# Attention over a graph: degree rows moved into the middle places, checks, roundings and loads of strips at fixed steps of the last place

## The chip, the cores and the metric

The kernel runs on one core of one Trainium2 chip. The metric is the device time of one execution in microseconds (us). The engines of a core are PE (TensorE: matmuls and transposes; PEld is its weight load), DVE (VectorE), ACT (ScalarE), POOL (GpSimd) and SP (SyncE, which here issues DMAs). Each engine works through its own queue in a fixed order, and an instruction that waits holds up those behind it on the same engine.

## The reference

Two layers on a graph of 2708 nodes with 128 features. `adj` is a 0/1 matrix of 2708 x 2708. Shortened:

```python
# layer 0
deg = clip(adj.sum(axis=1), 1.0);  dis = deg ** -0.5
diffusion = (dis[:, None] * adj * dis[None, :]) @ x - x
sim  = x @ x.T / (norms[:, None] * norms[None, :])
attn = softmax(beta * sim * adj, axis=1)
x = layernorm(x + diffusion + sigmoid(alpha) * (attn @ x - x))
# layer 1
XW = x @ W;  s_col = XW @ a[0, :128];  s_row = XW @ a[0, 128:]
den = exp(leaky_relu(s_row[:, None] + s_col[None, :], 0.01))
num = adj @ den
att = where(num != 0, den / num, 0)
x = layernorm(x + adj @ (att @ XW))
```

## The kernel before

The kernel has a version for adjacencies that a low precision holds exactly, `grouped` (which is what runs here), and a general one behind a condition. Whether the condition holds is found out on the way: ACT sums the absolute values of the low 16 bits of the adjacency's numbers (`low_bits_of`, `check_part`). These are the "checks".

Rows are handled in 22 blocks of 128, columns in strips of 512 (`SW`), six of them with the last one short (148, `SHORT`; strip number `NS - 1` = 5, the "side" strip). Row blocks lie in groups of four; group 5 has only two blocks.

**The attention part** (to about 219 us) walks five places, `for n, s in enumerate(order)` at L579 with `order = (2, 3, 4, 1, 0)`: place 0 works on strip 2, place 3 on strip 1 together with the side strip (it is the wide one), and place 4, the last, on strip 0. In each place there are 22 steps `k`, over row blocks in the order `taken`: blocks 8 to 21, then 4 to 7, then 0 to 3. So groups 2, 3, 4, 5, 1, 0 have their steps one after another. One step is:

- PE: `sim`, a matmul of 128 x 512 (or four transposes, where an earlier place has kept the turned block),
- DVE (L212 in the profile, a helper's line): `p_t = sim * gentle * pieces`, where `pieces` are blocks of the strip of the adjacency,
- ACT (L217): `p_t = exp(p_t + shift)`,
- POOL (L222): `total += p_t`, the softmax's denominators,
- PE (L207): `att_acc += x_sb^T p_t`, started one or more steps later. `p_t` has six buffers.

Beside the steps other work is laid into the loop:

- `degree(ib, h)`: half a block row of the adjacency is loaded by a DMA on SP into one of three rooms (`row0`, `row1`, and a part of `x1`), and ACT sums it by a copy with an accumulator (L198, `row<-row` or `x<-x`, 128 x 1354). There are 44 of these "degree rows"; `rows_at` says at which steps of which place they are asked for. `roots(b0, b1)` makes `dis` from them (DVE and POOL).
- `round_part(g)` at `rounded_at[g]` of the last place: DVE copies group g of strip 0 into the format fp32r for the diffusion.
- `check_part(g)` at `checked_at[g]` of the last place: the check of group g's numbers on ACT; its output, which nobody reads, goes into `row0` or `row1`, the same rooms that degree rows land in. Groups 1 and 0 are not in that table; they are checked later, in the diffusion's first pass, into a room of their own (`low_junk`).
- `load_part(1, g)`: POOL's queue asks for group g of strip 1 as fp32r, for the diffusion. It lands in the tile that held strip 0's group, so it stands behind what reads that one. At k = 17 and 20 of the last place groups 2 and 3 are asked for, the others in the diffusion's first pass.
- After steps 11, 15, 19 and 21 of the last place `x_sb` is scaled by `dis` on DVE (L742), for those blocks whose `att_acc` matmul lies behind. Then `halves` (L795) splits it into `x_hi` and `x_lo` (DVE, L212).

`pinned` chains instructions of one engine: each is put behind the last pinned one. `in_order(f)` sets the chain's end to the latest step's instruction (`behind`) and pins everything that `f` issues. What is not pinned is placed by a scheduler at compile time, by its own estimates of durations. Either way each engine's queue is fixed when the kernel is built, and rests on dependences through the rooms as well.

**The diffusion part** (to about 330 us) runs over strips, `for s in (NS - 1, 0, 1, 2)` at L1014 and then strips 3 and 4. `diffuse(s, acc)` is 22 x 2 matmuls on PE (`dif_acc<-strip,x_hi` and `dif_acc<-strip,x_lo`, L207; for the side strip `dif_acc<-side,x_sb`). `attended(s, acc, total)` closes a strip's attention: eight small matmuls make row sums of `total` (`sums`, L528), `att_acc` is copied to SBUF by ACT (`to_sbuf`) and turned on PE (`tr_ps`), and DVE divides and adds into `att`. For strip 0 this stands in the first pass, s = 5, that is between the side strip's diffusion and strip 0's. Afterwards each strip is normalized and layer 1's scores are made. Jobs of the next stage (`fill`) with their own loads (`nat`, issued by SP at L829) are laid in between from about 283 us. Layer 1 itself runs from about 345 us to the end.

Of the kernel before, what the change touches and what calls it, by code (L numbers as in the profile page):

```python
# [12 lines left out]
I16 = mybir.dt.int16  # L13
# [5 lines left out]
P = 128  # L19
N = 2708  # L20
D = 128
NB = (N + P - 1) // P
NP = NB * P
LAST = N - (NB - 1) * P
SW = 512
# [22 lines left out]
def grouped(  # L48
# [15 lines left out]
    nc = tc.nc  # L64
# [10 lines left out]
    def width(s):  # L75
        return min(SW, N - s * SW)

    def blocks(s):
        return min(SW // P, NB - s * (SW // P))
# [114 lines left out]
    def pinned(engine, op, *args, **kwargs):  # L194
        with ExitStack() as e:
            if engine in latest:
                e.enter_context(tc.issue_after(latest[engine].ins))
            latest[engine] = op(*args, **kwargs)  # L198
            return latest[engine]
# [14 lines left out]
    def act(op, *args, **kwargs):  # L214
        if strict:
            return pinned("ACT", getattr(nc.scalar, op), *args, **kwargs)
        return getattr(nc.scalar, op)(*args, **kwargs)  # L217

    def gps(op, *args, **kwargs):
        if strict:  # L220
            return pinned("POOL", getattr(nc.gpsimd, op), *args, **kwargs)
        return getattr(nc.gpsimd, op)(*args, **kwargs)  # L222
# [12 lines left out]
    def to_sbuf(acc, v, nb):  # L235

        t = lp.tile([P, SW], F32, tag="to_rows", name="tr_sb", bufs=2)
        if v < nb * P:
            nc.gpsimd.memset(t[:, v : nb * P], 0.0)
        act("copy", t[:, :v], acc[:, :v])  # L240
        return t
# [8 lines left out]
    def turned(t, nb):  # L250

        rows = tp_bank("tr_ps")
        for b in range(nb):
            mm(nc.tensor.transpose, rows[:, b, :], t[:, ts(b, P)], ident)
        return rows
# [38 lines left out]
    groups = list(dict.fromkeys(b // 4 for b in taken))  # L294
# [39 lines left out]
    with ExitStack() as es:  # L334
        pz = pool("pz", EARLY + 3, side="right", stack=es)
        pa = pool("pa", side="right", stack=es)
        row_rooms = [pa.tile([P, N // 2], F32, name=f"row{k}") for k in range(2)]
# [158 lines left out]
        def in_order(f):  # L496

            latest.update(behind)
            strict.append("some")
            f()  # L500
            strict.pop()
# [13 lines left out]
        def roots(b0, b1):  # L515

            t = deg[:, b0:b1]
            dve("tensor_tensor", t, deg2[:, b0:b1, 0], deg2[:, b0:b1, 1], ALU.add)
            dve("tensor_scalar", live[:, b0:b1], t, 0.0, None, ALU.is_gt)
            dve("tensor_scalar", t, t, 1.0, None, ALU.max)  # L520
            gps("tensor_tensor", dis[:, b0:b1], t, minus_half[:, b0:b1], ALU.pow)

        def attended(s, acc, total):

            v, nb = width(s), blocks(s)
            sums = tp_bank("sums")
            for b in range(nb):
                nc.tensor.matmul(  # L528
                    sums[:, b, 0:1], total[:, ts(b, P)], ones[:, 0:1], start=True, stop=True
                )  # L530
            rsum = small.tile([P, SW // P], F32, tag="rsum", name="rsum")
            nc.vector.reciprocal(rsum[:, :nb], sums[:, :nb, 0])
            nc.vector.tensor_scalar(rsum[:, :nb], rsum[:, :nb], sig, None, ALU.mult)
            rows = turned(to_sbuf(acc, v, nb), nb)
            for b in range(nb):
                ib = s * 4 + b
                r = att[:, ib, :]
                nc.vector.scalar_tensor_tensor(
                    r, rows[:, b, :], rsum[:, b : b + 1], r, ALU.mult, ALU.add
                )  # L540


        room_of = {2: "room5", 3: "room1", 4: "room3", 1: "room0", 0: "room4", 5: "room2"}
        rounded_at = {2: 5, 3: 8, 4: 12, 1: 15, 0: 18, 5: 19}
        checked_at = {2: 13, 3: 18, 4: 21, 5: 21}
        strips = {0: {}, NS - 1: kept_c}

        def part_of(s, g):
# [7 lines left out]
        def round_part(g):  # L556
            dve("tensor_copy", part_of(0, g), kept_a[g])

        def check_part(g, room=None):
            low_bits_of(  # L560
                kept_a[g].rearrange("p b i -> p (b i)"),
                room or row_rooms[g % 2].bitcast(I16),
            )

        def load_part(s, g):
            src = adj_t[4 * g * P : min(4 * g + 4, NB) * P, ts(s, SW)]
            pinned(
                "strips", gps, "dma_start", part_of(s, g),
                src.rearrange("(b p) i -> p b i", p=P),
            )  # L570
# [6 lines left out]
        ended = []  # L577
        scaled = set()
        for n, s in enumerate(order):  # L579
            wide = n == side_n  # L580
            w_all = SW + SHORT if wide else SW
            acc = ps_acc.tile([P, SW], F32, tag="acc", name="att_acc")
            if wide:
                total = x1[:, :6, :].rearrange("p b i -> p (b i)")
                nc.gpsimd.memset(total[:, w_all:], 1.0)
                tp_tags.remove("tp2")
                acc_side = ps_tp.tile([P, SW], F32, tag="tp2", name="att_acc_side")
            else:
                total = lp.tile([P, SW], F32, tag="total", name="total", bufs=2)
            gps("memset", total[:, :w_all], 0.0)  # L590

            prep = {
                (0, 1): lambda: normalize(12, 16),
# [6 lines left out]
                (1, 17): lambda: constants(2),  # L600
                (2, 11): lambda: roots(0, 8),
                (3, 20): lambda: roots(8, 18),
                (4, 12): lambda: roots(18, NB),
            }

            rows_at = {
                0: (18, 20), 1: range(0, NB, 2), 2: range(0, NB, 2),
                3: [k for k in range(21) if k % 3 < 2], 4: range(0, 12, 2),
            }
            turns = {  # L610
                3: lambda: turn_rows(12, 16, by_dve),
# [20 lines left out]
            for k, jb in enumerate(taken):  # L632
# [91 lines left out]
                if n == len(order) - 1:  # L724
                    for g in [g for g, at in rounded_at.items() if at == k]:
                        in_order(lambda: round_part(g))
                    if k in (17, 20):
                        in_order(lambda: load_part(1, groups[k > 17]))
                    for g in [g for g, at in checked_at.items() if at == k]:
                        in_order(lambda: check_part(g))  # L730
                    if k in (11, 15, 19, 21):

                        done = sorted(taken[: k + 1 if k == NB - 1 else k - 1])
                        done = [b for b in done if b not in scaled]
                        scaled.update(done)
                        while done:
                            b0 = b1 = done[0]
                            while b1 in done:
                                done.remove(b1)
                                b1 += 1  # L740
                            xs = x_sb[:, b0:b1, :]
                            nc.vector.tensor_tensor(  # L742
                                xs, xs,
                                dis[:, b0:b1].unsqueeze(2).to_broadcast([P, b1 - b0, D]),
                                ALU.mult,
                            )
# [8 lines left out]
    work2 = pool("work2", 2, stack=es)  # L755
# [6 lines left out]
    low = late.tile([P, NB], F32, name="low")  # L762
# [72 lines left out]
    for q in range(4):  # L835
        i, end = KEPT * SW + q * quarters[1], KEPT * SW + (q + 1) * quarters[1]
        c = 0
        while i < end:
            s = min(i // SW, NS - 1)
# [174 lines left out]
    for s in (NS - 1, 0, 1, 2):  # L1014
        acc = ps_acc.tile([P, SW], F32, tag="acc", name="dif_acc")
        diffuse(s, acc)
        if s < 3:
            load_strip(s + 2)
        if s == NS - 1:
            attended(*ended.pop())  # L1020
            for g in (1, 0):
                check_part(
                    g, work2.tile([P, 2048], I16, tag="low", name="low_junk", bufs=1)
                )
            for g in groups[2:]:
                load_part(1, g)
        if s == 1:
            flat = kept_c.rearrange("p b i -> p (b i)")
            v = SHORT
            for b0, b1 in ((0, NB // 2), (NB // 2, NB)):  # L1030
                low_bits_of(
                    flat[:, b0 * v : b1 * v],
                    work2.tile([P, 2048], I16, tag="low", name="low_junk", bufs=1),
                )
        normed(s, summed_up(s, acc))
        x1_t = x1_in_sbuf(s, x1_turned(s))
        pbs = []
        for k in (1, 0):
            pb = scores(s, x1_t, k, score_bank())
            tally(s, pb, k)  # L1040
            pbs.append(pb)
        shared_row(s, pbs[0])
        picked(s, pbs[0], sr_p)
        picked(s, pbs[1], sc_p)
        limited(s * 4, s * 4 + blocks(s))
        e2(s * 4, s * 4 + blocks(s))
        if s == 1:
            fill("e")

    r, s = NS - 3, NS - 2  # L1050
# [4 lines left out]
    acc = ps_acc.tile([P, SW], F32, tag="acc", name="dif_acc")  # L1055
# [70 lines left out]
    for name in "kj":  # L1126
        t = tmp.tile([P, 2, NB, 32], F32, tag=name + "_ons", name=name + "_ons")
# [402 lines left out]
    for step in range(NG + LAG):  # L1530
        g, before, first = step, step - 1, step - LAG
# [94 lines left out]
    k = 0  # L1626
# [568 lines left out]
```

## Time and profile before

| | us |
|---|---|
| median of 3 runs (lowest, highest) | 651.85 (651.62, 652.48) |
| the profiled execution: its own time | 652.04 |
| the profiled execution: span in the profile | 649.3 |

| engine | busy us | share of the span | instructions |
|---|---|---|---|
| PE | 608.8 | 94% | 2859 |
| DVE | 491.4 | 76% | 978 |
| ACT | 471.3 | 73% | 649 |
| POOL | 289.2 | 45% | 270 |

Times inside the profile are microseconds from the start of the span; a row of the timeline begins with the start and the duration. A duration in a row holds some pipelining, so that the distance between two starts is often a little shorter than the duration; such a distance is called a pitch here. "x10" at the end of a row is a number of instructions put together in one row; brackets tell how long the engine was idle before and who ended it. A name such as `row<-row` is the output tile and the input tiles. The mean granted clock of PE over the whole span was 0.984 of full speed. The places of the attention begin at about 10, 48, 92, 130 and 174 us.

### The profile page before, as it was taken

To read this page: it belongs to the slowest core of one execution; us is meant where nothing else is said; L and a number is where in the kernel's file an instruction comes from. 1 tells how busy PE (TensorE), PEld (TensorE's weight loads), DVE (VectorE), ACT (ScalarE), POOL (GpSimd) and SP (SyncE) were. 2 spreads that over 40 slices of the span, in tenths; PEclk is the share of its full clock that TensorE was granted. 3 is DMA by queue.
4 is the path that set the end of the run, shared out by engine and by line. 5 is a ranking of instruction groups with operands and counts; after the bars stand their busy time and mean duration, and the time that the engine had idled before them with its cause. 6 is when DMAs were issued, how large, how long until landed. Compare 5 with 4: busy or idle time off the path is not lost.

```text
span 649.3 us, 8555 instructions
## 1 busy us (share of the span) xinstructions
PE 608.8 (94%) x2859; PEld 351.9 (54%) x2859; DVE 491.4 (76%) x978; ACT 471.3 (73%) x649; POOL 289.2 (45%) x270
## 2 busy tenths in 40 slices
PE   7999999999999899998878899999999999989993
PEld 4445345465655676765664344444444444658872
DVE  5765865764699756756885999899999999599575
ACT  4767786767889521410585999999999999778652
POOL 6967778777798742000123322333232230021573
PEclk9999999999999899999988999999999999999997
DMA  8968989988971999989956999756689453259981
GB/s 270 392 221 330 317 301 363 360 329 310 335 262 70 276 390 389 387 267 375 394 205 185 238 223 246 214 168 175 193 217 267 170 170 129 87 202 383 390 320 53
DMA packets 66407, 171.64 MB, mean 264 GB/s; under 512 B 10059, under 2 KB 19285, under 8 KB 63333
## 3 DMA queue, kind: packets, MB, share of 16 engines
q1 hardware_dynamic: 42500, 107.01, 46.4%
q0 software_dynamic: 22464, 62.25, 34.5%
q10 hardware_dynamic: 1392, 1.77, 0.8%
q8 instruction: 24, 0.39, 0.2%
q14 instruction: 27, 0.21, 0.1%
HBM read 171.89 MB, written 5.72 MB: 274 GB/s over the span
## 4 chain that ended last, share of the span: by engine, by line
PE 65%; ACT 13%; DVE 10%; POOL 6%; issue 4%; DMA 1%; another core or an unknown queue 0%; DVEq 0%; POOLq 0%; ACTq 0%
PE num L198 11%; PE m_acc L198 11%; PE att_acc L207 9%; PE h_acc L1690 7%; PE sim L207 7%; PE dif_acc L207 6%; ACT q L198 5%; POOL total L222 4%; ACT L198 2%; DVE q L198 2%; PE tot L198 2%; PE dif_acc L198 1%; PE sim L198 1%; POOL ss L198 1%; ACT xn L198 1%
## 5 line engine op out<-in xcount | busy, mean ns | idle before, releaser
L198 PE MATMUL m_acc<-q,xws 128*128 128x512 f32 x240 | 121.6, 592 | 0.0
L198 PE MATMUL num<-ring,wt 128*128 128x512 f32 x216 | 98.2, 546 | 3.6 <-DVE q L198 2.2
L222 POOL TENSOR_TENSOR total<-total,p_t 128x512 f32<-128x512 f32 (+1 forms) x67 | 91.8, 1370 | 21.0 <-ACT p_t L217 18.4
L207 PE MATMUL att_acc<-p_t,x_sb 128*128 128x512 f32 x184 | 91.1, 602 | 1.1 <-ACT p_t L217 1.1
L212 DVE SCALAR_TENSOR_TENSOR p_t<-sim,gentle,pieces 128x512 f32<-128x512 f32 x89 | 65.0, 746 | 34.8 <-PE sim L207 25.7
L198 DVE SCALAR_TENSOR_TENSOR q<-sr_b,nc_s,q 128x1536 f32<-128x1536 f32 (+1 forms) x48 | 77.8, 1623 | 17.3 <-ACT q L198 17.3
L217 ACT ACTIVATE p_t<-p_t,shift 128x512 f32<-128x512 f32 (+1 forms) x89 | 64.7, 745 | 33.8 <-DVE p_t L212 31.5
L198 DVE COPY q<-num 128x512 f32<-128x512 f32 (+1 forms) x142 | 83.5, 611 | 4.5 <-PE num L198 4.5
L198 PEld LDWEIGHTS m_acc<-q,xws 128*128 128x128 f32 x240 | 45.3, 190 | 55.0 <-issue 54.8
L198 ACT ACTIVATE q<-q,head,rest 128x1536 f32<-128x1536 f32 (+1 forms) x48 | 70.2, 1508 | 1.6 <-DVE ring L198 1.3
L198 ACT ACT_TABLE_LOAD x52 | 66.7, 1283 | 3.9 <-issue 3.1
L198 PEld LDWEIGHTS num<-ring,wt 128*128 128x128 f32 x216 | 39.0, 190 | 49.1 <-issue 34.2
L198 ACT ACTIVATE q<-q,c_s 128x1536 f32<-128x1536 f32 (+1 forms) x48 | 62.9, 1355 | 0.3
L198 POOL DMA_INDIRECT ring<-in_adj_t,k_no x18 | 20.8, 1154 | 89.1 <-PE num L198 85.6
L207 PEld LDWEIGHTS att_acc<-p_t,x_sb 128*128 128x128 f32 x184 | 31.7, 189 | 35.3 <-ACT p_t L217 18.8
L207 PE MATMUL sim<-xn_t 128*128 128x512 f32 x98 | 47.6, 592 | 0.0
L222 POOL TENSOR_TENSOR x<-x,p_t 128x660 f32<-128x660 f32 (+1 forms) x22 | 35.1, 1596 | 11.3 <-ACT p_t L217 10.6
L198 ACT ACTIVATE row<-row 128x1354 f32<-128x1354 f32 x30 | 39.5, 1318 | 0.3 <-DMA row<-in_adj 0.3
L207 PE MATMUL dif_acc<-strip,x_hi 128*128 128x512 f32 x88 | 37.8, 429 | 0.0
L207 PE MATMUL dif_acc<-strip,x_lo 128*128 128x512 f32 x88 | 36.2, 411 | 0.0
L1690 PE MATMUL h_acc<-rounded,m_hi 128*128 128x512 f32 x88 | 32.4, 407 | 3.7 <-DVE rounded L212 3.7
L198 PE MATMUL num<-x_sb,wt 128*128 128x512 f32 (+1 forms) x72 | 34.4, 570 | 0.7 <-ACT gb L198 0.7
(362 smaller groups left out, 1170.6 us busy)
## 6 DMA issues: line engine op xcount, KB each, us to landing
pieces<-in_adj_t SPq DMA_DIRECT2D x24, 1024.0 KB, 6.8
strip<-in_adj_t POOLq DMA_DIRECT2D x20, 1024.0 KB, 18.3
row<-in_adj SPq DMA_DIRECT2D x30, 677.0 KB, 5.5
nat<-in_adj_t SPq DMA_DIRECT2D x19, 768.0 KB, 7.7
x<-in_adj SPq DMA_DIRECT2D x14, 677.0 KB, 6.2
ring<-in_adj_t SPq DMA_DIRECT2D x9, 1024.0 KB, 5.1
pieces<-in_adj_t SPq DMA_DIRECT2D x7, 512.0 KB, 6.4
x_sb<-in_adj_t SPq DMA_DIRECT2D x4, 768.0 KB, 6.2
```

The lines of the kernel that those rows point to most:

```text
L198: latest[engine] = op(*args, **kwargs)
L207: op(*args, **kwargs)
L212: return getattr(nc.vector, op)(*args, **kwargs)
L217: return getattr(nc.scalar, op)(*args, **kwargs)
L222: return getattr(nc.gpsimd, op)(*args, **kwargs)
L1690: nc.tensor.matmul(acc[:, : rows.shape[-1]], m[:, kb, :], rows, start=(kb, part) == (0, 0), stop=(kb, part) == (NB - 1, 1),)
```

## The change

- `rows_at`: place 1 asks for one more degree row (at k = 21), place 2 for two more (at k = 5 and 13), the last place for three instead of six (k = 0, 2, 4). `roots(18, NB)` goes from k = 12 to k = 7 of the last place.
- `rounded_at` is earlier by one step (group 5) to four steps (groups 4, 1 and 0).
- `checked_at` names all six groups, each at the step behind its rounding; the two checks with `low_junk` in the diffusion are gone, and `check_part` writes to `row0` or `row1` always.
- `asked_at` is new: all six groups of strip 1 are asked for at steps of the last place, each behind the group's check, in place of two there and four in the diffusion.
- The two `memset`s of the wide place's `total` are pinned.
- `attended` for strip 0 is called behind `diffuse(0)` instead of ahead of it; the copy of `att_acc` to SBUF stays ahead of it.

```diff
-        def attended(s, acc, total):
+        def attended(s, acc, total, t=None):
...
-            rows = turned(to_sbuf(acc, v, nb), nb)
+            rows = turned(t or to_sbuf(acc, v, nb), nb)
...
-        rounded_at = {2: 5, 3: 8, 4: 12, 1: 15, 0: 18, 5: 19}
-        checked_at = {2: 13, 3: 18, 4: 21, 5: 21}
+        rounded_at = {2: 3, 3: 5, 4: 8, 1: 11, 0: 14, 5: 18}
+        checked_at = {2: 4, 3: 6, 4: 9, 1: 12, 0: 15, 5: 19}
+        asked_at = {2: 9, 3: 10, 4: 13, 1: 16, 0: 19, 5: 21}
...
-        def check_part(g, room=None):
+        def check_part(g):
             low_bits_of(
                 kept_a[g].rearrange("p b i -> p (b i)"),
-                room or row_rooms[g % 2].bitcast(I16),
+                row_rooms[g % 2].bitcast(I16),
             )
...
-                nc.gpsimd.memset(total[:, w_all:], 1.0)
+                in_order(lambda: gps("memset", total[:, w_all:], 1.0))
...
-            gps("memset", total[:, :w_all], 0.0)
+            if wide:
+                in_order(lambda: gps("memset", total[:, :w_all], 0.0))
+            else:
+                gps("memset", total[:, :w_all], 0.0)
...
-                (4, 12): lambda: roots(18, NB),
+                (4, 7): lambda: roots(18, NB),
...
-                0: (18, 20), 1: range(0, NB, 2), 2: range(0, NB, 2),
-                3: [k for k in range(21) if k % 3 < 2], 4: range(0, 12, 2),
+                0: (18, 20), 1: (*range(0, NB, 2), 21), 2: (*range(0, NB, 2), 5, 13),
+                3: [k for k in range(21) if k % 3 < 2], 4: (0, 2, 4),
...
-                    if k in (17, 20):
-                        in_order(lambda: load_part(1, groups[k > 17]))
                     for g in [g for g, at in checked_at.items() if at == k]:
                         in_order(lambda: check_part(g))
+                    for g in [g for g, at in asked_at.items() if at == k]:
+                        in_order(lambda: load_part(1, g))
...
         if s == NS - 1:
-            attended(*ended.pop())
-            for g in (1, 0):
-                check_part(
-                    g, work2.tile([P, 2048], I16, tag="low", name="low_junk", bufs=1)
-                )
-            for g in groups[2:]:
-                load_part(1, g)
+            in_sbuf = to_sbuf(ended[0][1], SW, SW // P)
+        if s == 0:
+            attended(*ended.pop(), in_sbuf)
```

The compiled queues of the two kernels differ in this way around the last place. ACT: before, degree rows stand among steps 1 to 15, the check of group 2 ahead of step 16's exponential, that of group 3 behind step 18's, those of groups 4 and 5 behind step 21's. After, one row stands ahead of step 0, seven among steps 3 to 15; behind step 16's exponential stand the check of group 2, the last degree row, and the checks of groups 4, 3, 0 and 1; then the exponentials of steps 17 to 19, the check of group 5, and those of steps 20 and 21. DVE: behind step 21's product stand the scaling of blocks 18 to 21, that of blocks 4 to 7, seven of the splits, and the scaling of blocks 0 to 3. POOL: the asks for groups 2, 3, 4 and 1 stand between the additions of steps 16 and 17, that of group 0 behind step 19's, that of group 5 at the end. PE: strip 0's `att_acc` matmuls of steps 17 to 21 stand behind most of the side strip's diffusion; then the last side matmuls, strip 0's 44, and only then `sums`.

## The prediction

> **What bounds the kernel now.** I read the page's busy tenths first (PE, TensorE, near nine nearly everywhere, with a dent a third of the way in), then the busy time of each engine by windows. Columns: window, length, busy time and instructions of PE, its weight loads, DVE (VectorE), ACT (ScalarE) and POOL (GpSimd), granted clock, DMA share, GB/s.
>
> ```profile
> 48.00:92.00 44.00, 43.99 (x130) 20.44 (x129) 31.75 (x63) 32.83 (x51) 32.13 (x27) 1.00 0.87 310
> 92.00:130.00 38.00, 37.69 (x126) 19.16 (x125) 24.84 (x44) 27.73 (x43) 30.43 (x25) 1.00 0.99 359
> 186.00:200.00 14.00, 13.86 (x55) 7.52 (x55) 13.82 (x20) 13.39 (x21) 12.59 (x7) 1.00 0.71 237
> 200.00:210.00 10.00, 8.69 (x33) 4.82 (x31) 8.87 (x12) 10.00 (x13) 8.12 (x7) 1.00 0.00 0
> 210.00:218.60 8.60, 6.06 (x32) 4.39 (x32) 6.84 (x5) 4.74 (x9) 8.38 (x8) 1.00 0.52 132
> 231.00:270.00 39.00, 39.00 (x180) 28.09 (x179) 27.53 (x146) 11.45 (x18) 9.61 (x13) 1.00 1.37 388
> ```
>
> In the middle places PE is full and ACT has a quarter of its time free; in the second half of the last place ACT is full (10.00 of 10.00); from 219 on PE is full again. So work put into the middle is covered, and ACT work put into the last place is paid. Next, the chain of waits around the last place's end, then PE's own timeline there:
>
> ```profile
> 212.02 1.27 POOL total L222
> 217.28 1.29 POOL total L222
> 218.62 1.08 PE sums L528 x8
> 219.70 0.53 PE tr_ps L207 x2
> 220.23 4.28 PE dif_acc L207 x13
> ```
> ```profile
> 213.17 2.68 PE L207 MATMUL dif_acc<-side,x_sb 128*128 128x148 f32 x20
> 218.62 1.08 PE L528 MATMUL sums<-ones,total 128*128 128x1 f32 x8 [2.55 <-POOL total L222]
> 219.88 0.78 PE L207 MATMUL dif_acc<-strip,x_hi 128*128 128x512 f32 x1
> ```
>
> POOL's last addition lets `sums` go, and strip 0's diffusion starts at 219.88. From there to 272 the waits show PE waiting once, 0.7 us; the strip loads wait for PE (`POOL strip <- PE dif_acc`, 14.8 us in 10 waits). The loads after it are tied to PE as well (the queue at L829 waits 33.4 us for PE). I therefore carry a shift of 219.88 in full to the end.
>
> **The change part by part.** The diff alone would say "checks spread over the place". What decides is ACT's compiled queue, which is a fixed order. A check writes the room that degree rows land in, so it must stand behind every row ordered before it, and the queue still has nine of the 44 rows in the last place, the final one behind step 16. In the changed queue one row stands ahead of step 0, seven among steps 0 to 16, and no check; then stand, without an exponential between them: check of group 2, the last row, checks of groups 4, 3, 0, 1; then p17, p18, p19, the check of group 5, p20, p21 (p17 is step 17's exponential). Before, one check stood ahead of p16, one ahead of p19, two behind p21, and the two of groups 1 and 0 in the diffusion at 216.06 and 218.10. ACT's rows of before:
>
> ```profile
> 199.66 1.32 ACT L198 ACTIVATE row<-row 128x1354 f32<-128x1354 f32 x1
> 200.97 1.90 ACT L198 ACTIVATE row<-pieces 128x2048 int16<-128x2048 int16 x1
> 202.86 1.94 ACT L217 ACTIVATE p_t<-p_t,shift 128x512 f32<-128x512 f32 x3
> 204.70 1.90 ACT L198 ACTIVATE row<-pieces 128x2048 int16<-128x2048 int16 x1
> 206.60 1.93 ACT L217 ACTIVATE p_t<-p_t,shift 128x512 f32<-128x512 f32 x3
> 210.32 1.05 ACT L198 ACTIVATE row<-pieces 128x1024 int16<-128x1024 int16 x1
> ```
>
> Starts give the pitches: row 1.31, check 1.89, three exponentials 1.84 to 1.94, so 0.61 each; p17 started at about 203.5.
>
> *When p16 is ready.* Its product on DVE stood at 199.75 before. DVE now has one more rounding cast ahead (1.2) and spends 0.7 of idle time on it: about 200.3. ACT: p15 from 199.6, a row 1.32, p16 0.61, so free at 202.1. *The clump:* 1.89 + 1.32 + 4 x 1.89 = 10.77 us. p17 starts at 212.9, 9.4 later than before.
>
> *Behind p17.* Exponential and matmul 0.72 + 0.86, with 0.1 of hand-over; then DVE, whose next operation is the scaling of blocks 4 to 7 and which waits for that matmul, with the splitting into x_hi and x_lo queued behind it, though most blocks were long scaled. By before's rows:
>
> ```profile
> 213.37 0.69 DVE L742 TENSOR_TENSOR x_sb<-x_sb,dis 128x512 f32<-128x512 f32 x1 [1.76 <-PE att_acc L207]
> 213.97 2.90 DVE L212 CAST x_hi<-x_sb 128x384 fp32r<-128x384 f32 x2
> 216.80 2.92 DVE L212 TENSOR_TENSOR x_lo<-x_sb,x_hi 128x384 fp32r<-128x384 f32 x2
> 219.65 0.92 DVE L212 CAST x_hi<-x_sb 128x768 fp32r<-128x768 f32 x2
> 220.48 1.54 DVE L212 TENSOR_TENSOR x_lo<-x_sb,x_hi 128x768 fp32r<-128x768 f32 x2
> ```
>
> Scaling 0.69; the first four splits 5.7 (2.90 + 2.92 less overlap, beside POOL's additions, as they will again be); the next casts and a difference, which the queue puts ahead of the last scaling, 1.8 (the rows at 219.65 and 220.48, nothing beside them) to 3.6 (beside POOL, double); I take 2.4, nearer the first, since POOL is nearly through. Last scaling 0.69, the last four side matmuls 1.0 at 0.25. Sum 12.1: strip 0 starts at 225.0.
>
> *Moved work.* The row sums and two transposes (218.62 to 219.88, 1.26 us) now stand behind strip 0: still PE work, no gain. Strip 0's matmuls start 5.1 later, and what follows 5.1 + 1.26 = 6.4 later. Sums of totals cost no wait there: they are ready by about 222, and wanted after strip 0's 10 us; if not, 0 to 2.
>
> *The clock.* Before, PE idled 2.55 us, and strip 0's first matmuls ran at half clock:
>
> ```profile
> 220.00:221.00 1.00, 1.00 (x5) 0.81 (x4) 1.00 (x3) 0.97 (x3) 1.00 (x2) 0.50 1.27 420
> ```
>
> Seven matmuls at a pitch of 0.43 instead of 0.23 lost 1.4 us. Now there are two idle stretches, about 4 us ahead of p17's matmul and 4 to 5 us ahead of strip 0. The first falls where PE waits for others anyway; the second replaces the one of before. I add 0.4 for slower side matmuls and transposes between; bounds 0 and 1.4. [...]
>
> *At nothing.* Three rows more in middle places: 3 x 1.32 = 4.0 us of ACT under full PE (ACT 32.83 of 44 and 27.73 of 38). Their DMAs stand ahead of pieces on SP, where place two's share is 0.99; two rows are 1.39 MB, at 359 GB/s 3.9 us if that cover is gone, bounded at 0 and 3.9; I take 0, as pieces are asked for a place ahead, over 30 us. Memsets moved on POOL: under 1 us. Strip-1 asks: the four behind the clump wait for checks on POOL and delay additions; POOL issues each in 0.8 to 1.0, some 3.3 us, covered by strip 0, since nothing but the sums waits for totals. Earlier strips bring nothing while PE is the bound.
>
> Total: 6.4 + 0.4 = 6.8. The profiled execution has a span of 649.3 and took 652.04, 2.74 around it; 649.3 + 6.8 + 2.74 = 658.8, and the median lies 0.19 under that run: **658.6**.
>
> **The rivals.**
> **A, faster: ACT is quick enough.** ACT's work from p0 up to p17 is 17 x 0.61 + 8 x 1.31 + 5 x 1.89 = 30.3. Were p0 to start at 174.8 as before and nothing to wait, p17 would start at 205.1, strip 0 at 217.2, and with 1.26 moved behind it the end would come 1.4 earlier: 650.4; with p17 at 203.5, as before, 648.8. It decides when p17 starts ahead of 206.5 (206.5 + 12.1 + 1.26 = 219.9). Against: DVE was busy 13.82 of 14.00 us ahead of step 16, so p16 can't come 7 us earlier. 0.08.
> **B, no change: the checks run at their steps** (the rooms free sooner, or ACT idles less than I read): with the row now ahead of p0 and some idle time p0 starts at 176.6, p17 at 207.0, +0.5, 652.4. Against: the queue is fixed. 0.04.
> **C, strip 1's earlier loads repay it:** asks at about 204 to 213 instead of 211 to 222; if diffusion were fed by DMA (388 GB/s), up to 6 come back: 653 to 655. Against: PE full, 39.00 of 39.00. I give it 0.06 of the forecast's chance, at its lower end.
> [...] 0.12.
>
> **How the numbers follow.** Forecast 0.76, around 658.6. Its ends: with the splits unhindered (2.1 instead of 5.7), -3.6; with p17 1.2 earlier, another -1.2, so 653.8; I go to 653.5. Above: the slow differences +1.2, clock +1.0, part of the places' 3.9: 662.5. About 1 in 10 lies out on each side. This kernel's measurement can tell 0.2%, 1.3 us, from no change: faster 0.08 (A), same 0.04 (B), slower 0.88 (forecast and D).
>
> **What would show it.** Right: in ACT's timeline five checks and one row back to back from about 202 to 213, and p17 at 213; two idle stretches of PE, ahead of `att_acc` and ahead of the first `dif_acc<-strip` near 225; clock near 0.5 behind the second; `sums` behind strip 0. Wrong: p17 ahead of 206.5, exponentials between the checks, idle PE in places one and two, or PE waiting less in 225 to 330 than before.

## The result, and the profile after

| | before | after |
|---|---|---|
| median, us (lowest, highest; 6 runs each) | 651.74 (649.58, 652.93) | 658.81 (656.99, 663.03) |
| the profiled execution: its own time | 652.04 | 659.52 |
| the profiled execution: span | 649.3 | 657.8 |

The ratio of the times is 1.0124, 95% interval 1.0086 to 1.0161: the changed kernel is slower, by 7.1 us by the medians. Of the profiled executions the span is 8.5 longer and the own time 7.48, as 2.74 us lay around the span before and 1.72 after. One execution of each kernel is profiled. First the busy time by windows of the changed kernel, in the same columns as before.

```profile
92.00:130.00 38.00, 37.99 (x125) 19.12 (x124) 26.01 (x43) 28.42 (x44) 31.53 (x27) 1.00 0.97 358
186.00:200.00 14.00, 13.67 (x59) 7.97 (x60) 13.22 (x19) 10.79 (x17) 13.45 (x9) 1.00 0.71 251
200.00:213.00 13.00, 10.01 (x42) 6.74 (x40) 7.01 (x11) 13.00 (x17) 11.16 (x10) 0.89 0.29 80
213.00:226.00 13.00, 8.29 (x22) 4.43 (x22) 10.48 (x11) 4.43 (x8) 9.51 (x11) 0.76 1.28 364
```

Place 2 (92 to 130) is as full on PE as before, so the rows put there cost nothing. In 186 to 200 ACT even has 3.2 us free (13.39 busy before, 10.79 now). Then it turns: in 200 to 213 ACT is busy for all of 13.00 us and PE lacks 3.0; in 213 to 226 PE lacks another 4.7, and its clock is 0.76. ACT's timeline says what it did in 200 to 213:

```profile
201.25 0.71 ACT L217 ACTIVATE p_t<-p_t,shift 128x512 f32<-128x512 f32 x1
201.87 1.89 ACT L198 ACTIVATE row<-pieces 128x2048 int16<-128x2048 int16 x1
203.76 1.32 ACT L198 ACTIVATE row<-row 128x1354 f32<-128x1354 f32 x1
205.07 1.90 ACT L198 ACTIVATE row<-pieces 128x2048 int16<-128x2048 int16 x1
...
210.75 1.89 ACT L198 ACTIVATE row<-pieces 128x2048 int16<-128x2048 int16 x1
212.65 1.93 ACT L217 ACTIVATE p_t<-p_t,shift 128x512 f32<-128x512 f32 x3
```

The `row<-pieces` operations are the checks. Between step 16's exponential and step 17's stand five checks and the last degree row, back to back. What PE made of it, in its own timeline:

```profile
210.84 2.34 PE L207 MATMUL dif_acc<-side,x_sb 128*128 128x148 f32 x8 [2.99 <-DVE x_sb L746]
213.41 6.27 PE L207 MATMUL att_acc<-p_t,x_sb 128*128 128x512 f32 x10 [0.22 <-ACT p_t L217]
...
225.17 2.34 PE L207 MATMUL dif_acc<-side,x_sb 128*128 128x148 f32 x8 [4.49 <-DVE x_sb L746]
227.13 0.81 PE L207 MATMUL dif_acc<-strip,x_hi 128*128 128x512 f32 x1
...
240.32 0.94 PE L528 MATMUL sums<-ones,total 128*128 128x1 f32 x8
```

The brackets hold the two waits, 2.99 and 4.49 us. Strip 0's diffusion starts at 227.13 (219.88 before), and the row sums stand behind it, at 240.32. DVE's rows between these two waits:

```profile
215.52 1.44 DVE L746 TENSOR_TENSOR x_sb<-x_sb,dis 128x512 f32<-128x512 f32 x1 [4.73 <-PE att_acc L207]
216.88 3.70 DVE L212 CAST x_hi<-x_sb 128x384 fp32r<-128x384 f32 x2
220.50 2.34 DVE L212 TENSOR_TENSOR x_lo<-x_sb,x_hi 128x384 fp32r<-128x384 f32 x2
...
224.44 0.68 DVE L746 TENSOR_TENSOR x_sb<-x_sb,dis 128x512 f32<-128x512 f32 x1
```

DVE stood idle for 4.73 us ahead of the scaling that waits for step 17's matmul, with the splits queued behind it.

A milestone that serves for all runs below is the start of the last `x_lo` matmul of strips 0 to 2, which PE works through almost without a wait: 273.1 before, 281.6 after, so 8.5 later.

### The profile page after: what moved, and what is told of

Read it like the earlier page. It is cut to its first block, busy times and chain, and to the rows that moved or that the text cites. A ratio compares the mean times of both kernels' runs of the same rounds, so it can differ in the third digit from the quotient of the medians.

```text
span 657.8 us, 8552 instructions
## 1 busy us (share of the span) xinstructions
PE 614.5 (93%) x2859; PEld 356.9 (54%) x2859; DVE 495.7 (75%) x978; ACT 473.6 (72%) x651; POOL 292.0 (44%) x270
## 4 chain that ended last, share of the span: by engine, by line
PE 76%; DVE 10%; ACT 6%; issue 4%; POOL 2%; DMA 2%; another core or an unknown queue 0%; DVEq 0%; ACTq 0%; POOLq 0%
PE num L198 16%; PE m_acc L198 16%; PE att_acc L207 10%; PE h_acc L1690 7%; PE sim L207 7%; PE dif_acc L207 7%; ACT row L198 2%; PE tot L198 2%; PE dif_acc L198 1%; DMA x<-in_adj 1%; PE sb_ps L207 1%; PE sim L198 1%; POOL ss L198 1%; ACT xn L198 1%; PE att_acc L198 1%
## 5 line engine op out<-in xcount | busy, mean ns | idle before, releaser
L198 DVE COPY q<-num 128x512 f32<-128x512 f32 (+1 forms) x142 | 85.7, 615 | 11.5 <-PE num L198 11.2
L207 PE MATMUL att_acc<-p_t,x_sb 128*128 128x512 f32 x184 | 92.5, 612 | 1.2 <-ACT p_t L217 1.2
L198 POOL DMA_INDIRECT xws<-xw_d,j_no x24 | 29.9, 1246 | 14.5 <-DVE c_s L198 7.5
```

## The experiments

Ratios are to the kernel before, run on the same chip beside them (median 650.5 to 650.9 us there). "Milestone" is the one above.

### Short checks and half checks

```diff
             low_bits_of(
-                kept_a[g].rearrange("p b i -> p (b i)"),
+                kept_a[g].rearrange("p b i -> p (b i)")[:, :128],
 (second run)
-                kept_a[g].rearrange("p b i -> p (b i)"),
+                kept_a[g][:, : (g < 5) + 1, :].rearrange("p b i -> p (b i)"),
```

> The changed kernel, but each check reads only 128 numbers a partition of its group in place of 2048 (1024 for group 5); so most of the adjacency goes unchecked. ACT's queue keeps its order. Theory (the time of the five checks between steps 16 and 17 on ACT is the loss): the clump shrinks from 10.8 us to the row's 1.3 and five short instructions of about 0.3, 2.8 in all, step 17's exponential starts at about 204.7 in place of 212.65, strip 0's diffusion at about 219, and the time falls by 8 to about 651. Rival (the loss comes from the sums behind strip 0, the loads of strip 1 or the degree rows in the middle places): 657 to 660, as the changed kernel.

> The changed kernel, but each check reads half of its group (1024 numbers a partition, 512 for group 5); half of the adjacency goes unchecked. Same order on ACT. Theory: five checks at 1.04 in place of 1.89 (the pitch of the 1024-wide check), 4.25 less ahead of step 17, and about as much off the time: step 17 at 208.4, time about 654.5, halfway between the short checks and the full ones. Rival (a threshold: once the exponential waits at all, the clock falls and the loss is fixed): within 1.5 of the changed kernel. Rival of the other causes: 657 to 660.

Short checks: 650.72 us, ratio 1.0014 (0.9993 to 1.0034), no difference from before; milestone 273.0. Half checks: 655.34 us, ratio 1.0084 (1.0046 to 1.0122); milestone 275.3. ACT's and PE's timeline with the short checks:

```profile
201.72 0.30 ACT L198 ACTIVATE row<-pieces 128x128 int16<-128x128 int16 x1
...
204.50 1.94 ACT L217 ACTIVATE p_t<-p_t,shift 128x512 f32<-128x512 f32 x3
```
```profile
219.01 0.81 PE L207 MATMUL dif_acc<-strip,x_hi 128*128 128x512 f32 x1
```

The clump goes from 10.78 us (201.87 to 212.65) to 2.78, step 17 starts 8.15 us earlier and strip 0 8.12 us earlier. With half checks step 17 starts at 208.26, and the bulk of strip 0 at 222.79 (two of its matmuls run from 219.43 on). ACT's order was the same in the three kernels, only the checks' length differs. By the ratios the loss goes from 1.24% to 0.84% with the half checks and to 0.14%, no loss, with the short ones. So the length of the checks is shown to be the cause of the loss, and neither the sums, the rows nor the early loads, which these runs kept, are needed for it. A loss that is fixed once the exponential waits is not borne out; the intervals of half and full checks overlap.

From step 17's exponential to strip 0 it is 14.5 us in all three (227.13 - 212.65, 219.01 - 204.50, 222.79 - 208.26), but this is a coincidence, as the path is not the same. PE with half checks:

```profile
211.63 2.34 PE L207 MATMUL dif_acc<-side,x_sb 128*128 128x148 f32 x8 [3.90 <-DVE x_sb L746]
213.76 4.92 PE L207 MATMUL att_acc<-p_t,x_sb 128*128 128x512 f32 x10
```

Step 17's matmul did not wait for ACT here but stands behind side matmuls, which waited for DVE's scaling by `dis` (POOL made it at 208.91). So DVE's next scaling, which waits for that matmul, began at 215.29, only 0.23 us earlier than in the changed kernel (215.52), although the exponential started 4.4 us earlier. Strip 0 gained its 4.3 us behind that: the first four splits took 4.4 us instead of 5.9, while POOL's additions ended 2 us earlier; the compiled order has the last scaling ahead of the next three splits (1.7); and the last side matmuls ran at full clock (1.0). With the short checks, too, the chain into strip 0 runs over POOL's `dis` (208.88) and not over step 17. In the changed kernel itself this second path was 0.22 us shorter than ACT's: that is all that step 17's matmul waited for ACT.

### The old steps of checks and loads; the checks alone

```diff
 (the changed kernel)
-        checked_at = {2: 4, 3: 6, 4: 9, 1: 12, 0: 15, 5: 19}
-        asked_at = {2: 9, 3: 10, 4: 13, 1: 16, 0: 19, 5: 21}
+        checked_at = {2: 13, 3: 18, 4: 21, 5: 21}
+        asked_at = {2: 17, 3: 20}
...
         if s == NS - 1:
             in_sbuf = to_sbuf(ended[0][1], SW, SW // P)
+            for g in (1, 0):
+                check_part(
+                    g, work2.tile([P, 2048], I16, tag="low", name="low_junk", bufs=1)
+                )
+            for g in groups[2:]:
+                load_part(1, g)
 (second run: the kernel before)
-        rounded_at = {2: 5, 3: 8, 4: 12, 1: 15, 0: 18, 5: 19}
-        checked_at = {2: 13, 3: 18, 4: 21, 5: 21}
+        rounded_at = {2: 3, 3: 5, 4: 8, 1: 11, 0: 14, 5: 18}
+        checked_at = {2: 4, 3: 6, 4: 9, 1: 12, 0: 15, 5: 19}
+        asked_at = {2: 9, 3: 10, 4: 13, 1: 16, 0: 19, 5: 21}
 (and the checks and loads of the diffusion's first pass go, as in the change)
```

> The changed kernel with the old steps of checks and of strip 1's loads: checks of groups 2, 3, 4 and 5 at steps 13, 18, 21 and 21, groups 1 and 0 in the diffusion's first pass, loads as before; the degree rows, the early roundings and the sums behind strip 0 stay changed. Theory: step 17 at about 205.3 (one check and one row ahead of it), strip 0's diffusion at 218.3 to 219.5, the 1.26 us of sums behind it: 651 to 652.5. Rival (rows, roundings or sums make the loss): 656 to 660. Rival (earlier loads of strip 1 had been a gain): over 653.

> The kernel before with the change's steps for roundings, checks and loads of strip 1 alone; degree rows, roots and sums as before. Theory (what counts is ACT's whole work ahead of the last exponential): before, two full checks stood ahead of it and it ended at 208.5; now five full ones and a short one, 3 x 1.89 + 1.04 = 6.7 more, so it ends at about 215 (216.8 in the changed kernel), and the time is 6 to 8 above before, the whole loss. Rival (rows or sums have a share): under 4 above before.

With the old steps in the changed kernel: 650.77 us, ratio 1.0021 (0.9992 to 1.0050); milestone 271.2; step 17 at 205.00, where 205.3 was expected. The new steps alone on the kernel before: 659.22 us, ratio 1.0134 (1.0099 to 1.0170); milestone 279.2; the last exponential ended at 216.8, as in the changed kernel, where 215 was expected. So undoing the steps of checks and loads takes the whole loss away, and the new steps of roundings, checks and loads alone bring the whole loss. In the second kernel the checks are not in one clump (two stand behind step 11, one behind step 14, two behind step 15), which says that the clump is not needed for the loss. All five still stand ahead of step 17, which starts at 212.6; but step 17's matmul again stands behind side matmuls that waited for a scaling (211.27), so how much of the loss came over ACT's queue is not shown.

The short checks kept the early loads of strip 1, this kernel had the late ones, and their ratios (1.0014 and 1.0021) are not told apart: the early loads bring nothing that these runs can measure, though the two kernels differ in their checks as well.

### A room of their own for the checks

```diff
+        check_room = pa.tile([P, 2 * SW], I16, name="check_room")
...
-            low_bits_of(
-                kept_a[g].rearrange("p b i -> p (b i)"),
-                row_rooms[g % 2].bitcast(I16),
-            )
+            for b in range(0, min(4, NB - 4 * g), 2):
+                low_bits_of(
+                    kept_a[g][:, b : b + 2, :].rearrange("p b i -> p (b i)"), check_room
+                )
 (in the second run also: groups 1 and 0 taken out of the two tables,
  checked and loaded in the diffusion's first pass)
```

> The changed kernel, but the checks write to a room of their own, which no degree row uses. It has room for 1024 numbers, so each check is made in two halves (two instructions of 1.04 in place of one of 1.89, 0.95 us more in all). ACT's compiled queue then has the checks spread over steps 5 to 19, at the table's steps, none in a clump. Theory (the clump comes from the shared rooms, and without it ACT's work from step 0 on, 22 x 0.61 + 8 x 1.31 + 11 x 1.04 = 35.3, fills its time): step 17 at 207.8 if ACT never waits, 210.5 with the waits of before; time 654 to 657, better than the changed kernel but no gain over before. Rival (spread checks cost nothing, the clump alone does): about 651. Rival (total work on ACT counts, not its place): 659 or more.

> The run with a room of their own for the checks, but groups 1 and 0 are checked in the diffusion's first pass as before (and their loads follow there). Theory (ACT's whole work ahead of the last exponential sets the end of the place, clump or no clump): 4 x 1.04 = 4.2 less of it, the last exponential ends at about 212 in place of 216.2, time 4 below that run, 653.5 to 655. Rival (the spread checks failed because PE waited 4.0 us for a scaling in another order): within 1.5 of that run, 657 to 659.

The first: 658.23 us, ratio 1.0122 (1.0080 to 1.0165); milestone 281.0. The second: 657.95 us, ratio 1.0114 (1.0080 to 1.0149); milestone 278.8. Both expectations of the theory missed; in the second the rival's 657 to 659 came. Step 17 did come earlier (208.81 in the first, within the 207.8 to 210.5 expected), and yet the bulk of strip 0 did not (227.31 in the first); in the second the last exponential ended only at 219.1, where 212 was expected. PE's timeline of the second run shows another wait:

```profile
203.08 1.81 PE L207 MATMUL dif_acc<-side,x_sb 128*128 128x148 f32 x6 [4.04 <-DVE x_sb L747]
```

In these two queues PE has matmuls of the side strip ahead of the products of later steps, and they wait for a scaling, which on DVE stands behind a rounding; both took about three microseconds (3.16 and 3.04, against 1.21 and 1.90 in the changed kernel). POOL adds beside them in both kernels, here with asks for strips between; what made the difference is not shown. So these runs do not tell whether spread checks would be cheaper than clumped ones: the compiled order changed on three engines with the edit. What stays open is the price of a spread with everything else in place.

### One scaling instead of two; the sums first again

```diff
-                    if k in (11, 15, 19, 21):
+                    if k in (11, 15, 21):
 (second run)
-            in_sbuf = to_sbuf(ended[0][1], SW, SW // P)
-        if s == 0:
-            attended(*ended.pop(), in_sbuf)
+            attended(*ended.pop())
```

> The changed kernel, but blocks 4 to 7 are scaled by dis together with blocks 0 to 3 at step 21, not by an operation of their own that waits for step 17's matmul. So on DVE the splitting of blocks 8 to 21 no longer stands behind that wait. Theory (behind the clump, DVE's queue adds a second loss, the splits waiting for step 17 though their blocks are ready): splitting begins at about 213 in place of 216.9, largely ahead of POOL's additions; the last scaling then waits for step 21's matmul (219.7); strip 0's diffusion at about 222.5 in place of 227.1, time 4 to 5 below the changed kernel, 653 to 655. Rival (the splits wait for ACT's rooms or are slowed by POOL whenever they run): within 1.5 of the changed kernel.

> The changed kernel with the row sums and transposes of strip 0's attention ahead of its diffusion again. Theory (PE has 4.5 us idle there, and POOL's last addition ends at 221.7, before the wait for the scaling ends at 225.2): the 1.26 us fall into that idle time and leave the stretch behind strip 0; strip 0 starts as in the changed kernel, at about 227, and what follows comes 1.3 earlier: 657 to 658. Rival (the move behind strip 0 was a gain, as sums would hold PE until POOL is done): 659.5 or more.

One scaling: 656.03 us, ratio 1.0116 (1.0059 to 1.0173); the interval holds the changed kernel's ratio, so the time is inconclusive; the milestone, 279.9, is 1.7 earlier, where the theory had strip 0 and the time 4 to 5 earlier. The reason is in DVE's timeline of that run:

```profile
215.36 1.11 DVE L212 CAST x_hi<-x_sb 128x640 fp32r<-128x640 f32 x1 [4.41 <-ACT row L198]
```

The first cast ran at 210.59, but the second waited for ACT's check of group 5, which ended at 215.2. So the splits wait for the checks in two ways, by step 17's matmul and by a check; freeing one leaves the other. The rival was half right.

Sums first: 657.98 us, ratio 1.0112 (1.0073 to 1.0152); milestone 281.6, as in the changed kernel. The run tells little: in the compiled order PE still has seven matmuls of strip 0 ahead of the sums (they run at 230.83). Whether the sums in PE's idle stretch would save the 1.26 us was not tested by it.

### The degree rows alone; all checks behind the place

```diff
 (the kernel before)
-                0: (18, 20), 1: range(0, NB, 2), 2: range(0, NB, 2),
-                3: [k for k in range(21) if k % 3 < 2], 4: range(0, 12, 2),
+                0: (18, 20), 1: (*range(0, NB, 2), 21), 2: (*range(0, NB, 2), 5, 13),
+                3: [k for k in range(21) if k % 3 < 2], 4: (0, 2, 4),
...
-                (4, 12): lambda: roots(18, NB),
+                (4, 7): lambda: roots(18, NB),
 (second run: the changed kernel)
-        checked_at = {2: 4, 3: 6, 4: 9, 1: 12, 0: 15, 5: 19}
-        asked_at = {2: 9, 3: 10, 4: 13, 1: 16, 0: 19, 5: 21}
+        checked_at = {}
+        asked_at = {}
...
             in_sbuf = to_sbuf(ended[0][1], SW, SW // P)
+            for g in groups:
...
+                room = work2.tile([P, 2048], I16, tag="low", name="low_junk", bufs=1)
+                check_part(g, room)
+                load_part(1, g)
```

> The kernel before with only the degree rows and the roots moved as in the change; checks, roundings, loads of strip 1 and sums as before. Theory (rows in places 1 and 2 are hidden under PE): no loss there, and ACT in the last place has three rows less, so step 17 up to 3 earlier; strip 0's start is held by DVE and POOL, so 0 to 2 us below before. Rival (place 2's DMA share of 0.99 and SP's queue): PE waits in place 2, 1 to 4 above before.

> The changed kernel with all six checks, and behind each the load of strip 1's group, in the diffusion's first pass: the checks stand behind step 21's exponential on ACT and write to the room that groups 1 and 0 used before. Nothing is left out. Theory (checks on ACT cost only where exponentials wait behind them; ACT has 27 of 39 us free in the diffusion): step 17 at about 203, last exponential by 206 to 207, strip 0 at 216.5 to 219, 1 to 3 us below before. Rival (strip 1's groups come too late, as each load waits for its check): PE waits for strip 1 at about 232, 2 or more above before.

Rows alone: 649.24 us, ratio 0.9983 (0.9968 to 0.9998), a small gain, barely clear of none; PE in place 2 is busy for 37.99 of 38.00 us, without a wait. Checks behind the place: 652.28 us, ratio 1.0025 (1.0004 to 1.0045), a small loss, as barely clear, milestone 275.3; the theory expected a gain. Step 17 did start at about 203, but at the last two steps ACT then waited for DVE and POOL (3.45 and 4.12 us), and strip 0 started at 220.89. Taking checks off the place stops paying when ACT is no longer what the last steps wait for.

### The casts on ACT

```diff
-        halves(x_part(0, b0, b1), x_part(1, b0, b1), x_sb[:, b0:b1, :])
+        act("copy", x_part(0, b0, b1), x_sb[:, b0:b1, :])
+        dve(
+            "tensor_tensor", x_part(1, b0, b1), x_sb[:, b0:b1, :], x_part(0, b0, b1),
+            ALU.subtract,
+        )
 (both runs; beside it the edit of the rows, and of the old steps, as above)
```

> The kernel before with the degree rows and the roots moved as in the change, and the casts to x_hi made by ACT in place of DVE. Theory (beside POOL's additions the casts on DVE took 3.9 us where they took 0.95 alone; ACT is not slowed so): x_hi done at about 217 in place of 218.5, x_lo a little earlier; strip 0 is held by the sums too, so 0 to 1 below the run with rows alone, 0.2% to 0.4% below before. Rival (ACT's checks of groups 4 and 5 stand ahead of the casts): no gain over rows alone, or a loss of 1 to 2.

> The run with the old steps of checks and loads (rows, roundings and sums changed), and the casts to x_hi made by ACT in place of DVE. Theory: in that run strip 0's first x_lo waited 2.4 us for DVE; with the casts off DVE it starts at about 217 without that wait, 1.5 to 2.5 below that run, 0.1% to 0.3% below before. Rival (POOL's additions slow the subtraction as much, or ACT's checks come first): as that run, no difference from before.

With the rows moved: 648.29 us, ratio 0.9959 (0.9938 to 0.9980), faster than both kernels; milestone 271.2 (272.3 with the rows alone). On the run with the old steps: 649.73 us, ratio 0.9982 (0.9962 to 1.0002), not told apart from before; milestone 269.6 against 271.2 without the edit. The first rows of the casts, on DVE in the run with the rows alone, then on ACT:

```profile
214.69 3.88 DVE L212 CAST x_hi<-x_sb 128x384 fp32r<-128x384 f32 x2
```
```profile
215.69 2.91 ACT L217 CAST x_hi<-x_sb 128x384 fp32r<-128x384 f32 x5
```

Two casts on DVE beside POOL's additions took 3.88 us; all five took 2.91 on ACT. The share of the casts in the 0.41% is not shown apart from the rows' share, since the two intervals overlap.

## Why the prediction was right

Forecast 658.6, measured 658.81, on the way that was forecast in its main part, the clump; the nearness of the two numbers is luck, as shown below. Step by step:

| step | predicted | measured |
|---|---|---|
| ACT free behind p16 | 202.1 | 201.87 |
| five checks and a row, us | 10.77 | 10.78 |
| p17 starts | 212.9 | 212.65 |
| p17 to strip 0, us | 12.1 | 14.5 |
| strip 0 starts | 225.0 | 227.13 |
| sums behind strip 0, us | 1.26 | 1.25 (8.5 at the milestone, 7.25 at strip 0) |
| shift, to the end | 6.8 | 8.5 at the milestone and in the span, 7.48 in the execution's time |

**The clump** was right in its place, order and size, and the runs with short and half checks show the length of its checks to be the cause. What the prediction did not see is the second path to the same matmul, over POOL's `dis`, DVE's scaling and the side matmuls at half clock (0.50 from 211 to 213.4): in the changed kernel it ends 0.22 us ahead of ACT's, so that p17 does set the time there, but a shorter clump does not bring DVE's scaling forward us for us.

**The tail behind p17** was 2.4 us too small. Taken apart: exponential and matmul to 215.50 took 2.85 (1.68 predicted), the scaling 1.36 (0.69), the four splits 5.88 (5.7), the next three 1.68 (2.4), the last scaling 0.7, the side matmuls 1.96 (1.0). Of the excess of 1.17 and 0.96 at the two matmul steps most is the half clock, at which the matmul of step 17 took 2.08 us (1.13 for two such at full clock in the run with the rows alone) and the last side matmuls 1.96 (1.0 at full clock in the run with half checks): PE's clock fell to 0.50 twice, in the idle stretches of 2.99 and 4.49 us, and this hit the path itself. I had put the clock at 0.4 because the first fall "falls where PE waits for others anyway"; that step failed: step 17's matmul was what DVE waited for. The other excess, 0.67 at the scaling, and the 0.72 too much for the three splits behind it cancel.

**What made the total look better than its terms.** Three errors cancel. The span grew by 8.5, not 6.8, so 1.7 was missing. I had kept 2.74 us around the span; in all six executions of the changed kernel only 1.6 to 1.7 lay there, 1.0 less. And the median lies 0.71 below the profiled execution, where I took 0.19: another 0.5 less. What is left, 0.2, is luck, and the interval of the ratio, 5.6 to 10.5 us of loss, is far wider.

Nor did the 8.5 of the milestone stay as it was. The last totals before layer 1 stand 8.0 later, the first `m_acc` matmul only 6.3, because in the profiled executions the kernel before ran layer 1's first matmuls at half clock and the changed one did not (its first four `num` matmuls took 3.65 us, against 1.98). The first `h_acc` matmul stands 5.8 later; there it is the changed kernel that runs at half clock (a pitch of 0.43 against 0.23), and the last ask for output stands 7.45 later. The remaining 1.0 of the span lies behind that ask, and the same 1.0 is missing around the span. Whether the two stretches at half clock belong to the kernels or to the executions is not shown: one execution of each is profiled, and over 340 to 360 us the mean clock was 0.91 in the run with the old steps and 1.00 in the same run with the casts on ACT. So the carry "in full to the end" came out in the sum, 8.5 at the milestone and 8.5 in the span, but not step by step.

**The rivals.** A (ACT is quick enough) was priced at 650.4 for p17 at 205.1. With short checks p17 came at 204.50, for which its sum gives a gain of 2.0, and the time was that of before (ratio 1.0014, at best 0.5 us below): the tail was too short in that price too. Where the sign turns is not shown, as strip 0 then waits for another chain. B (the checks at their steps: 652.4) is not borne out as far as it could be tried: both runs with spread checks took 658, though through another wait. C (the early loads repay up to 6) is not borne out: with and without them the ratios are not told apart, within some 3 us. A time above the forecast's range, for which the prediction kept 0.12, did not come: the clock fell twice, to 0.50 at 210.1 and at 223.7, but place 2 lost nothing (PE busy for 37.99 of 38.00 us).

**At nothing.** The rows in the middle places cost nothing, as said; moved alone in the kernel before they even gave 0.17% (barely clear of none), which I had not counted.

## What to carry to other kernels

Read the compiled queue of the engine that is full, not the step numbers in the code: a step that shares a buffer with lagging work runs when that work is done, and here five checks met in one place. A stall of one engine should be priced to the end of the chain behind it, and against the other paths that end at the same instruction, with PE at half clock around an idle stretch, as here around those of 2.99 and 4.49 us, if PE's work is on that chain. Work that nobody waits for (a check) can be free only where nothing that is waited for stands behind it in the same queue.

## What the runs showed of the hardware

PE's granted clock fell to 0.50 in or just behind idle stretches of 2.55 us (before) and of 2.99 and 4.49 us (after). Read in windows of 0.2 us, it fell at 219.5 and was back at 222.9 before; after, it fell at 210.1, was back at 216.9, fell at 223.7 and was back at 230.5. So the half clock lasted 3.4, 6.8 and 6.8 us, and in the changed kernel each step lies 6.8 us behind the last. Three other runs agree, by an estimate from their mean clocks: 0.87 over 213 to 226 with the short checks, 0.93 and 0.94 over 200 to 213 and 213 to 226 with the half checks, and 0.95 and 0.92 over the same two windows with the checks behind the place come to 3.4 us at half clock each. The length of an idle stretch alone did not settle it: behind one of 1.83 us the 26 side matmuls took 4.68 us in the run with the rows moved and the casts on ACT, and 3.44 behind one of 1.83 in the run with the rows alone, where the clock was 1.00; in the run with the old steps one of 2.38 passed at 1.00. What sets these steps of the clock is not shown.

Two casts on DVE took 3.88 us beside POOL's additions in the run with the rows alone, and 0.95 ahead of POOL's next addition in the run with the short checks; all five took 2.91 on ACT in the run with the rows moved.

ACT's check took 0.30 us for 128 numbers a partition (short checks), 0.61 for 512 and 1.04 for 1024 (half checks) and 1.89 for 2048 (the changed kernel): by an estimate from these some 0.2 us and 0.83 per 1024, so that splitting a check in two costs only 0.19.
